# Cross-attention on one Trainium2 core: the audio projection as block products of eleven passes, with the output normalisation spread over the batch

## The chip, the cores and the metric

The kernel runs on one core of one Trainium2 chip. The metric is the device time of a whole execution in microseconds (us); less is better. TensorE (PE) multiplies matrices, VectorE (DVE), ScalarE (ACT) and GpSimd (POOL) do the elementwise work, and SyncE (SP) issues nearly all DMAs from one queue, in order. All numbers are float32.

## What is computed

There are 64 batches. Each has text rows `x` (256 rows of 512) and audio rows `c` (256 rows of 384). The reference, cut to what matters (`H_l` is `x`, `H_a` is `c`):

```python
text_p  = einsum('bld,dh->blh', H_l, W_text)  + b_text     # 512 x 512 weights
audio_p = einsum('bsd,dh->bsh', H_a, W_audio) + b_audio    # 384 x 512 weights
Q = layer_norm(text_p,  g1, beta1)
K = layer_norm(audio_p, g2, beta2)
V = audio_p
alpha = softmax(einsum('blh,bsh->bls', Q, K) / sqrt(512), axis=-1)
H = einsum('bls,bsh->blh', alpha, V)
H = einsum('blh,hk->blk', H, W_out) + b_out
return layer_norm(H + H_l, g_out, beta_out)
```

## The kernel before

The engines run the instructions in the order in which the program lists them; the order of the loop body is written out by hand, and no scheduler reorders it. An engine that waits holds back everything behind it in its own list. Tiles come from pools with a fixed number of buffers, and a new tile waits until the one whose buffer it takes over is done with. [...]

**One batch.** The rows are loaded twice: as rows (`load_rows`, for the residual and as V) and in squares of 32 columns (`load_squares`), which VectorE turns into `xT` and `cT` (`turn_x`, `turn_c`). The text projection is a class `Blocks`: a 2 x 2 block product in seven products instead of eight (Strassen's idea in Winograd's form). GpSimd forms sums of input blocks (`sum_x`, four a batch) and, once at the start, sums of weight blocks (`weight_sums`). TensorE runs the products two to a bank (`products`), and VectorE puts them together (`leave`), one instruction for each product. Each text product takes two matmuls with 256 result columns, so fourteen in all. The audio projection is a plain `Projection`: two row tiles of three matmuls each with 512 result columns (`multiply`), and one eviction for each tile (`evict`). ScalarE squares the rows for the variance, GpSimd makes the inverse root (`scales`), ScalarE scales the rows (`normalise`). The result is stored to DRAM (`store`) and fetched back in squares (`fetch`), VectorE turns it (`turn`), and ScalarE applies the layer norm's weights (`affine`).

The scores are eight matmuls of 256 columns. VectorE takes the row maximum and multiplies it by minus the scale (`maxima`), and ScalarE takes exponentials. These go to DRAM and back (`store_e`, `fetch_e`) and are turned in the next batch (`turn_e`). `context` multiplies them by `c`, six matmuls of 256 columns. The output product uses W_audio times W_out, which is multiplied together once at the start: two tiles of three matmuls of 512 columns. `evict` adds the residual, to which GpSimd has added the output bias (`add_bias`), and takes the statistics; `finish` normalises, two VectorE instructions for each of two row tiles.

**The loop** is a pipeline. In the pass for batch b the scores are those of b, the projections belong to b+2, context and output to b-1 (`last`), and the final normalisation to b-2 (`done`). The input squares of b+3 are turned in the same pass. Batches 0 and 1 are projected ahead of the loop, in the plain form for both sides, and the last two batches end behind it.

Of the kernel before, what the change touches and what calls it, by code (L numbers as in the profile page):

```python
# [9 lines left out]
F32 = mybir.dt.float32  # L10
AF = mybir.ActivationFunctionType
ALU = mybir.AluOpType
# [10 lines left out]
def kernel(  # L23
# [36 lines left out]

    nc = tc.nc
    ctx.enter_context(tc.manual_schedule())
    B, L, D = x.shape
# [10 lines left out]
    work = ctx.enter_context(tc.tile_pool(name="work", bufs=2))  # L76
    small = ctx.enter_context(tc.tile_pool(name="small", bufs=4))
    scratch = ctx.enter_context(tc.tile_pool(name="scratch", bufs=3, space=bass.MemoryType.DRAM))
    p_pj = ctx.enter_context(tc.tile_pool(name="p_pj", bufs=3, space=PSUM))
    p_at = ctx.enter_context(tc.tile_pool(name="p_at", bufs=3, space=PSUM))  # L80
    p_y = ctx.enter_context(tc.tile_pool(name="p_y", bufs=2, space=PSUM))

    def squares(dst, src):
# [68 lines left out]
    def take_columns():  # L152

        ps = p_at.tile([P, P], F32, tag="at", name="ps_v")
        nc.tensor.transpose(ps, vectors, ident)
        nc.scalar.copy(columns, ps[:, : 5 * HC].rearrange("p (n k) -> p n k", n=5))
        return [columns[:, n, :] for n in range(5)]
# [89 lines left out]
        for k in range(n):  # L247
            nc.vector.tensor_scalar(rows[:, k, :], rows[:, k, :], mv[:, k, 0:1], None, ALU.subtract)

    HALF = DC // 2  # L250
    H2 = H // 2

    def weight_sums():

        w = [[wt_sb[:, j * HALF : (j + 1) * HALF, k * H2 : (k + 1) * H2] for k in (0, 1)] for j in (0, 1)]
        t = const.tile([P, 4, HALF, H2], F32, tag="wsum", name="wsum")
        add = nc.gpsimd.tensor_tensor
        add(t[:, 0], w[0][1], w[0][0], ALU.subtract)
        add(t[:, 1], w[1][1], t[:, 0], ALU.subtract)
        add(t[:, 2], w[1][1], w[0][1], ALU.subtract)  # L260
        add(t[:, 3], w[1][0], t[:, 1], ALU.subtract)
        return {1: w[0][0], 2: w[1][0], 3: w[1][1], 4: t[:, 3], 5: t[:, 0], 6: t[:, 1], 7: t[:, 2]}

    def rstd_of(var, n):
        ve = small.tile([P, n], F32, tag="ve", name="ve")
# [5 lines left out]
    class Projection:  # L271


        def __init__(self, name, b, srcT, w_sb, bias, nch, nt):
            self.name, self.b, self.nt, self.nch = name, b, nt, nch
            self.srcT, self.w_sb, self.bias = srcT, w_sb, bias
            self.rows = work.tile([P, nt, H], F32, tag=f"{name}r", name=f"{name}r_{b}")
            self.centred = b > 1
            if not self.centred:
                self.mv = small.tile([P, nt, 2], F32, tag=f"mv{name}", name=f"mv{name}")  # L280
            self.ps = {}
# [96 lines left out]
    class Blocks(Projection):  # L378
# [3 lines left out]

        def __init__(self, b, xT, sums):
            super().__init__("q", b, xT, None, bt_sb, DC, LT)
            part = lambda i, j: xT[:, j * HALF : (j + 1) * HALF, bass.ts(i, P)]
            self.side = {
                1: part(0, 0), 2: part(0, 1), 4: part(1, 1),
                5: sums[:, 0], 6: sums[:, 1], 7: sums[:, 2], 3: sums[:, 3],  # L390
            }

        def products(self, *ns):

            bank = p_pj.tile([P, 2, H2], F32, tag="pj", name="ps_q")
            for j, n in enumerate(ns):
                self.ps[n] = bank[:, j : j + 1, :]
                for k in range(HALF):
                    nc.tensor.matmul(  # L399
                        bank[:, j, :],  # L400
                        lhsT=self.side[n][:, k, :],
                        rhs=blocks_of_wt[n][:, k, :],
                        start=(k == 0),
                        stop=(k == HALF - 1),
                    )

        def leave(self, n):
# [22 lines left out]
    class Attention:  # L430
# [14 lines left out]
                    )  # L445

        def maxima(self):
            mx = small.tile([P, LT], F32, tag="mx", name="mx")
            nc.vector.tensor_reduce(mx, self.sc, AX.X, ALU.max)
            self.nmx = small.tile([P, LT], F32, tag="nmx", name="nmx")  # L450
            nc.vector.tensor_scalar(self.nmx, mx, -scale, None, ALU.mult)

        def exponentials(self):

            self.e = work.tile([P, LT, S], F32, tag="e", name=f"e_{self.b}")
            self.den = small.tile([P, LT], F32, tag="den", name="den")
            for t in range(LT):
                nc.scalar.activation(  # L458
                    self.e[:, t, :],
                    self.sc[:, t, :],  # L460
                    AF.Exp,
                    bias=self.nmx[:, t : t + 1],
                    scale=scale,
                    accum_out=self.den[:, t : t + 1],
                )

# [73 lines left out]
        def scales(self, lo=0, n=LT):  # L540
            self.r = {lo + t: r for t, r in enumerate(rstd_of(self.mv[:, lo : lo + n, 1], n))}

        def finish(self, lo=0, n=LT):
            y = self.y
            for t in range(lo, lo + n):
                nc.vector.scalar_tensor_tensor(  # L546
                    y[:, t, :], y[:, t, :], self.mv[:, t, 0:1], go_sb, ALU.subtract, ALU.mult
                )
                nc.vector.scalar_tensor_tensor(  # L549
                    y[:, t, :], y[:, t, :], self.r[t], beo_sb, ALU.mult, ALU.add  # L550
                )

        def store(self, lo=0, n=LT):
            nc.sync.dma_start(
# [3 lines left out]

    def text(b, xT):
        return Projection("q", b, xT, wt_sb, bt_sb, DC, LT)  # L560

    def sum_x(xT):

        part = lambda i, j: xT[:, j * HALF : (j + 1) * HALF, bass.ts(i, P)]
        s = work.tile([P, 4, HALF, P], F32, tag="xsum", name="xsum")
        add = nc.gpsimd.tensor_tensor
        add(s[:, 0], part(1, 0), part(1, 1), ALU.add)
        add(s[:, 1], s[:, 0], part(0, 0), ALU.subtract)
        add(s[:, 2], part(0, 0), part(1, 0), ALU.subtract)
        add(s[:, 3], part(0, 1), s[:, 1], ALU.subtract)  # L570
        return s

    def audio(b, cT):
        return Projection("k", b, cT, wa_sb, ba_sb, AC, ST)
# [43 lines left out]
    q[0].scales()  # L618
    k[0].fetch()
    g1_sb, be1_sb, g2_sb, be2_sb, bac_sb = take_columns()  # L620
    waT = turn_weights()
    q[0].normalise()
    q[0].store()
# [8 lines left out]
    q[0].fetch()  # L632
    k[1].store()
    blocks[2] = load_squares(2)
    k[0].turn()
    k[0].affine(g2_sb, be2_sb)
    q[1] = text(1, xT.pop(1))
# [15 lines left out]
    fold_evict(1)  # L653
    fold_multiply(2)
    fold_evict(2)
    blocks_of_wt = weight_sums()
    xT[2] = turn_x(2)
    sums = {2: sum_x(xT[2])}
    for v, name in ((bt_sb, "mbt"), (ba_sb, "mba")):
        v = v.rearrange("p (o h) -> p o h", o=1)  # L660
        centre(v, means(v, 1, name), 1)
    blocks[3] = load_squares(3)
    bao_sb = fold_bias(part)
    centre(wa_sb, mean_wa, AC)
    cT[2] = turn_c(2)
    go_sb = row(g_out, "go")
    beo_sb = row(beta_out, "beo")

    done = last = None
    for b in range(B - 2):  # L670
        three = b + 3 < B
        at = Attention(b)
        if b:
            q[b + 1].fetch()
            k[b + 1].normalise()
            k[b + 1].store()
        at.scores()
        if done:
            done.evict(1)
            done.scales()  # L680
        if last:
            last.turn_e()
        at.maxima()
        at.exponentials()
        at.store_e()
        k[b + 1].fetch()
        at.fetch_e()
        if b + 4 < B:
            blocks[b + 4] = load_squares(b + 4)
        rows[b + 1] = load_rows(b + 1)  # L690
        add_bias(b)
        text_2 = q[b + 2] = Blocks(b + 2, xT.pop(b + 2), sums.pop(b + 2))
        text_2.products(1, 2)
        text_2.leave(1)
        text_2.products(6, 5)
        text_2.leave(6)
        text_2.leave(2)
        text_2.leave(5)
        text_2.products(7, 3)
        q[b + 1].turn()  # L700
        q[b + 1].affine(g1_sb, be1_sb)
        at.reciprocals()
        if last:
            last.context()
        if done:
            done.finish()
            done.store()
        text_2.leave(3)
        text_2.leave(7)
        k[b + 2] = audio(b + 2, cT.pop(b + 2))  # L710
        k[b + 2].multiply(0)
        text_2.products(4)
        k[b + 2].evict(0)
        text_2.leave(4)
        text_2.square()
        text_2.scales()
        k[b + 1].turn()
        k[b + 1].affine(g2_sb, be2_sb)
        if three:
            xT[b + 3] = turn_x(b + 3)  # L720
        if last:
            last.start_output()
            last.multiply(0)
        text_2.normalise()
        text_2.store()
        if three:
            sums[b + 3] = sum_x(xT[b + 3])
        k[b + 2].multiply(1)
        if last:
            last.evict(0)  # L730
        if three:
            cT[b + 3] = turn_c(b + 3)
        k[b + 2].evict(1)
        k[b + 2].square()
        k[b + 2].scales()
        if last:
            last.multiply(1)
        done, last = last, at


    at = Attention(B - 2)
    q[B - 1].fetch()
    k[B - 1].normalise()
    k[B - 1].store()
    rows[B - 1] = load_rows(B - 1)
    at.scores()
    done.evict(1)
# [1 line left out]
    last.turn_e()  # L749
    at.maxima()  # L750
    at.exponentials()
    k[B - 1].fetch()
    add_bias(B - 2)
    last.context()
    at.reciprocals()
# [73 lines left out]
```

## Time and profile before

| | |
|---|---|
| time, median of 3 runs | 1482.82 us (1482.72 to 1484.9) |
| the profiled execution | 1483.51 us, span 1481.7 us |
| TensorE busy | 1457.2 us (98%) |
| VectorE busy | 1147.0 us (77%) |
| ScalarE busy | 723.0 us (49%) |
| GpSimd busy | 525.4 us (35%) |
| DMA share of 16 engines, mean moved | 73.8% on the main queue, 217 GB/s |
| granted TensorE clock | 0.997 |

The busy time of an engine is the union of its instructions. TensorE's matmuls overlap in the records and their ends are modelled, so the start of a group is a safer mark than its end. One float32 matmul of the program leaves two records. In lines of the profile, `L399` is a line of the kernel, followed by the engine, the operation, and output and inputs under the program's names.

### The profile page before, as it was taken

The page shows a single profiled execution, that of the slowest core. Times are in us where ns is not written, and L with a number is a line of the kernel's source. Part 1 is how long each engine was busy: PE and PEld are TensorE (multiplying, and loading weights), DVE is VectorE, ACT ScalarE, POOL GpSimd, SP SyncE. Part 2 cuts the span into 40 slices and gives each one's busy share as a digit, 9 for nine tenths or more (in the row PEclk, how much of TensorE's full clock was granted, in tenths as well). Part 3 has the DMA queues.
Part 4 walks back from the last instruction along what each step waited for, and adds up shares of the span by engine and source line. Part 5 has one row for each costly group of instructions (what it writes and reads, how often), then busy time and mean ns, then how long its engine had stood idle before and what let it go on. Part 6 is the DMA issues. An engine that isn't in the chain of part 4 may idle for free.

```text
span 1481.7 us, 18230 instructions
## 1 busy us (share of the span) xinstructions
PE 1457.2 (98%) x5157; PEld 978.4 (66%) x5157; DVE 1147.0 (77%) x1829; ACT 723.0 (49%) x1663; POOL 525.4 (35%) x785
## 2 busy tenths in 40 slices
PE   7999999999999999999999999999999999999997
PEld 3566676676676676676676676676766766766763
DVE  5867877777877877877877877878778778778777
ACT  2444545545545544545545545445445445455452
POOL 1434334334334334334333333343343343343332
PEclk9999999999999999999999999999999999999999
DMA  8777777777778777877777777777777777777752
GB/s 192 179 218 226 217 224 219 223 230 220 220 241 232 221 220 232 227 217 224 223 221 219 216 234 224 218 232 226 218 228 228 213 228 234 212 223 222 227 190 81
DMA packets 450248, 322.27 MB, mean 217 GB/s; under 512 B 154724, under 2 KB 382564, under 8 KB 450148
## 3 DMA queue, kind: packets, MB, share of 16 engines
q1 hardware_dynamic: 449328, 319.79, 73.8%
q10 hardware_dynamic: 820, 1.32, 0.5%
q8 instruction: 41, 0.67, 0.2%
q14 instruction: 59, 0.48, 0.1%
HBM read 204.09 MB, written 116.92 MB: 217 GB/s over the span
## 4 chain that ended last, share of the span: by engine, by line
PE 94%; DMA 2%; DVE 2%; issue 1%; ACT 1%; SPq 0%; POOL 0%; POOLq 0%; DVEq 0%
PE ps_q L399 24%; PE ps_y L521 21%; PE ps_k L286 21%; PE ps_sc L439 14%; PE ps_z L504 11%; PE ps_q L286 1%; PE ps_wao L214 1%; DMA c<-in_ctx_dram 0%; DMA qd<-qr 0%; SPq L87 0%; DMA wt<-in_L_xattn_W_text_dram 0%; DMA bt<-in_L_xattn_b_text_dram 0%; DVE y L549 0%; DVE y L546 0%; DMA ed<-e 0%
## 5 line engine op out<-in xcount | busy, mean ns | idle before, releaser
L286 PE MATMUL ps_k<-wa,cT 128*128 128x512 f32 x768 | 353.0, 596 | 1.0 <-DMA wa<-in_L_xattn_W_audio_dram 1.0
L521 PE MATMUL ps_y<-wao,zT 128*128 128x512 f32 x768 | 350.4, 592 | 1.0 <-ACT zT L511 0.9
L266 POOL TENSOR_SCALAR ve<-var 128x2 f32<-128x2 f32 x124 | 27.1, 218 | 725.4 <-ACT junk L304 725.4
L286 PEld LDWEIGHTS ps_k<-wa,cT 128*128 128x128 f32 x768 | 146.5, 191 | 157.8 <-issue 138.4
L521 PEld LDWEIGHTS ps_y<-wao,zT 128*128 128x128 f32 x768 | 145.6, 190 | 157.8 <-issue 151.4
L414 DVE TENSOR_TENSOR qr<-ps_q,qr 128x512 f32<-128x512 f32 x372 | 184.5, 510 | 76.1 <-PE ps_q L399 71.8
L370 ACT ACTIVATE qT<-qT,columns 128x256 f32<-128x256 f32 x256 | 132.9, 590 | 222.3 <-DVE qT L90 212.6
L439 PE MATMUL ps_sc<-kT,qT 128*128 128x256 f32 x1024 | 233.7, 381 | 3.3 <-ACT kT L370 3.3
L439 PEld LDWEIGHTS ps_sc<-kT,qT 128*128 128x128 f32 x1024 | 195.1, 191 | 58.6 <-issue 27.5
L458 ACT ACTIVATE e<-ps_sc,nmx 128x256 f32<-128x256 f32 x128 | 59.6, 470 | 241.9 <-PE ps_q L399 229.3
L504 PE MATMUL ps_z<-eT,c 128*128 128x256 f32 x768 | 176.3, 379 | 0.7 <-ACT eT L493 0.7
L530 DVE SCALAR_TENSOR_TENSOR y<-ps_y,rden,x 128x512 f32<-128x512 f32 x128 | 93.5, 731 | 103.8 <-PE ps_y L521 102.7
L399 PE MATMUL ps_q<-wsum,xsum 128*128 128x256 f32 x744 | 170.7, 379 | 0.0
L589 POOL TENSOR_TENSOR x<-x,bao 128x512 f32<-128x512 f32 x128 | 160.3, 1274 | 4.6 <-DMA x<-in_x_dram 4.5
L504 PEld LDWEIGHTS ps_z<-eT,c 128*128 128x128 f32 x768 | 145.8, 190 | 21.1 <-ACT eT L493 0.9
L399 PEld LDWEIGHTS ps_q<-wsum,xsum 128*128 128x128 f32 x744 | 141.4, 190 | 19.2
L370 ACT ACTIVATE kT<-kT,columns 128x256 f32<-128x256 f32 x256 | 132.9, 590 | 38.8 <-DVE kT L363 33.7
L268 POOL TENSOR_TENSOR rstd<-ve,nhalf 128x2 f32<-128x2 f32 (+1 forms) x193 | 136.6, 708 | 16.1
L304 ACT ACTIVATE junk<-qr 128x512 f32<-128x512 f32 x124 | 78.1, 630 | 112.5 <-DVE qr L414 112.5
L399 PE MATMUL ps_q<-wt,xT 128*128 128x256 f32 x496 | 117.2, 379 | 0.0
L332 ACT ACTIVATE kr<-kr,rstd 128x512 f32<-128x512 f32 x124 | 82.8, 714 | 70.1 <-POOL rstd L268 70.1
L549 DVE SCALAR_TENSOR_TENSOR y<-y,rstd,beo 128x512 f32<-128x512 f32 x128 | 97.1, 758 | 11.5 <-POOL rstd L268 2.5
(95 smaller groups left out, 1698.1 us busy)
## 6 DMA issues: line engine op xcount, KB each, us to landing
x<-in_x_dram SPq DMA_DIRECT2D x64, 512.0 KB, 5.0
kd<-kr SPq DMA_DIRECT2D x64, 512.0 KB, 3.3
kq<-kd SPq DMA_DIRECT2D x256, 128.0 KB, 2.7
qd<-qr SPq DMA_DIRECT2D x64, 512.0 KB, 4.9
qq<-qd SPq DMA_DIRECT2D x256, 128.0 KB, 2.6
xq<-in_x_dram SPq DMA_DIRECT2D x252, 128.0 KB, 2.8
out_dram<-y SPq DMA_DIRECT2D x63, 512.0 KB, 6.0
c<-in_ctx_dram SPq DMA_DIRECT2D x64, 384.0 KB, 5.3
```

The source lines that it names most:

```text
L268: nc.gpsimd.tensor_tensor(r, ve, nhalf[:, :n], ALU.pow)
L286: nc.tensor.matmul(ps, lhsT=self.srcT[:, k, bass.ts(t, P)], rhs=self.w_sb[:, k, :], start=(k == 0), stop=(k == self.nch - 1),)
L332: nc.scalar.mul(row, row, self.r[t])
L370: nc.scalar.activation(self.T[:, k, :], self.T[:, k, :], AF.Identity, bias=bet[:, k : k + 1], scale=gam[:, k : k + 1],)
L399: nc.tensor.matmul(bank[:, j, :], lhsT=self.side[n][:, k, :], rhs=blocks_of_wt[n][:, k, :], start=(k == 0), stop=(k == HALF - 1),)
L414: add = lambda o, i0, i1: nc.vector.tensor_tensor(o, i0, i1, ALU.add)
L439: nc.tensor.matmul(self.sc[:, t, :], lhsT=self.qT[:, k, bass.ts(t, P)], rhs=self.kT[:, k, :], start=(k == 0), stop=(k == HC - 1),)
L504: nc.tensor.matmul(ps[:, j, :], lhsT=self.c_sb[:, s, bass.ts(lo + j, P)], rhs=self.eT[:, s, :], start=(s == 0), stop=(s == ST - 1),)
L521: nc.tensor.matmul(ps, lhsT=self.zT[:, k, bass.ts(t, P)], rhs=wao_sb[:, k, :], start=(k == 0), stop=(k == AC - 1),)
L530: nc.vector.scalar_tensor_tensor(self.y[:, t, :], self.ps_y.pop(t), self.rden[:, t : t + 1], self.xb[:, t, :], ALU.mult, ALU.add,)
L549: nc.vector.scalar_tensor_tensor(y[:, t, :], y[:, t, :], self.r[t], beo_sb, ALU.mult, ALU.add)
L589: nc.gpsimd.tensor_tensor(xb[:, t, :], xb[:, t, :], bao_sb, ALU.add)
```

## The change

It has four parts.

1. The audio projection from batch 2 on uses `Blocks` as well. The first two of its three chunks of 128 input columns form the 2 x 2 block product, with one matmul for each of the seven products. The third chunk's plain product with `W_audio` has four quarters; each is added by one more matmul to a product that goes to just that quarter of the result (2, 3, 4 and 5). That makes eleven matmuls of 256 columns where there were six of 512. The new `sum_c` makes the sums of input blocks on GpSimd; the sums of weight blocks are made ahead of the loop.
2. `finish` is split into `shift` and `settle` for each row tile, and the four instructions are spread between the maximum and the text evictions.
3. The score's scale goes into the key's layer norm weights ahead of the loop, so that the maximum is negated by the reduction itself and its second small instruction goes.
4. The order changes: all seven text products run ahead of the context, the audio product runs in one piece behind it, and the two output tiles follow each other. The keys of a batch are normalised and stored at the end of the pass instead of at the top of the next, and fetched ahead of the exponentials' store. `add_bias` moves from the top to the middle of the pass. The pools change to four banks for `p_pj` and two for `p_at`.

The core of the diff; the parts of `Blocks` that only take other names are left out.

```diff
-    p_pj = ctx.enter_context(tc.tile_pool(name="p_pj", bufs=3, space=PSUM))
-    p_at = ctx.enter_context(tc.tile_pool(name="p_at", bufs=3, space=PSUM))
+    p_pj = ctx.enter_context(tc.tile_pool(name="p_pj", bufs=4, space=PSUM))
+    p_at = ctx.enter_context(tc.tile_pool(name="p_at", bufs=2, space=PSUM))
...
+    def sum_c(cT):
+        part = lambda i, j: cT[:, j, bass.ts(i, P)]
+        s = work.tile([P, 5, P], F32, tag="csum", name="csum")
+        add = nc.gpsimd.tensor_tensor
+        add(s[:, 0], part(1, 0), part(1, 1), ALU.add)
+        add(s[:, 1], s[:, 0], part(0, 0), ALU.subtract)
+        add(s[:, 2:4], cT[:, 0:3:2, :P], cT[:, 0:3:2, P:], ALU.subtract)
+        add(s[:, 4], part(0, 1), s[:, 1], ALU.subtract)
+        return {
+            1: [part(0, 0)], 2: [part(0, 1), part(0, 2)], 4: [part(1, 1), part(1, 2)],
+            5: [s[:, 0], part(1, 2)], 6: [s[:, 1]], 7: [s[:, 2]], 3: [s[:, 4], s[:, 3]],
+        }
...
         def products(self, *ns):
-            bank = p_pj.tile([P, 2, H2], F32, tag="pj", name="ps_q")
+            bank = p_pj.tile([P, 2, H2], F32, tag="pj", name=f"ps_{self.name}")
             for j, n in enumerate(ns):
                 self.ps[n] = bank[:, j : j + 1, :]
-                for k in range(HALF):
+                pairs = list(zip(self.sides[n], self.weights[n]))
+                for i, (side, w) in enumerate(pairs):
                     nc.tensor.matmul(
...
+                        bank[:, j, :], lhsT=side, rhs=w, start=(i == 0), stop=(i == len(pairs) - 1)
                     )
...
         def maxima(self):
-            mx = small.tile([P, LT], F32, tag="mx", name="mx")
-            nc.vector.tensor_reduce(mx, self.sc, AX.X, ALU.max)
             self.nmx = small.tile([P, LT], F32, tag="nmx", name="nmx")
-            nc.vector.tensor_scalar(self.nmx, mx, -scale, None, ALU.mult)
+            nc.vector.tensor_reduce(self.nmx, self.sc, AX.X, ALU.max, negate=True)
...
+        def shift(self, t):
+            nc.vector.scalar_tensor_tensor(
+                self.y[:, t, :], self.y[:, t, :], self.mv[:, t, 0:1], go_sb, ALU.subtract, ALU.mult
+            )
+
+        def settle(self, t):
+            nc.vector.scalar_tensor_tensor(
+                self.y[:, t, :], self.y[:, t, :], self.r[t], beo_sb, ALU.mult, ALU.add
+            )
...
+    for v in (g2_sb, be2_sb):
+        nc.vector.tensor_scalar(v, v, scale, None, ALU.mult)
...
     blocks[2] = load_squares(2)
+    k[1].fetch()
...
     centre(wa_sb, mean_wa, AC)
+    wa_blocks = weight_sums(wa_sb, 1, "wasum")
+    for n, k2 in ((2, 0), (3, 1), (5, 1), (4, 0)):
+        wa_blocks[n].append(wa_sb[:, 2, k2 * H2 : (k2 + 1) * H2])
     cT[2] = turn_c(2)
+    cs = {2: sum_c(cT[2])}
```

The loop body after the change, for batch b (lines that only stand under `if` for the first and last passes are written without it):

```python
q[b + 1].fetch()
k[b + 1].fetch()
at.scores()
done.evict(1)
done.scales()
done.shift(0)
last.turn_e()
at.maxima()
done.shift(1)
at.exponentials()
at.store_e()
at.fetch_e()
blocks[b + 4] = load_squares(b + 4)
rows[b + 1] = load_rows(b + 1)
q2 = q[b + 2] = Blocks("q", b + 2, xs.pop(b + 2), wt_blocks, bt_sb)
q2.products(1, 2)
q2.leave(1)
done.settle(0)
q2.products(6, 5)
q2.leave(6)
q2.leave(2)
q2.leave(5)
q2.products(7, 3)
q[b + 1].turn()
q[b + 1].affine(g1_sb, be1_sb)
q2.products(4)
q2.leave(3)
q2.leave(7)
q2.leave(4)
at.reciprocals()
last.context()
q2.square()
done.settle(1)
done.store()
q2.scales()
add_bias(b)
k[b + 1].turn()
k[b + 1].affine(g2_sb, be2_sb)
q2.normalise()
q2.store()
k2 = k[b + 2] = Blocks("k", b + 2, cs.pop(b + 2), wa_blocks, ba_sb)
k2.products(1, 2)
k2.leave(1)
k2.products(6, 5)
k2.leave(6)
k2.leave(2)
k2.leave(5)
k2.products(7, 3)
k2.leave(3)
k2.leave(7)
k2.products(4)
k2.leave(4)
k2.square()
k2.scales()
last.start_output()
last.multiply(0)
xT[b + 3] = turn_x(b + 3)
xs[b + 3] = sum_x(xT.pop(b + 3))
cT[b + 3] = turn_c(b + 3)
cs[b + 3] = sum_c(cT.pop(b + 3))
k2.normalise()
k2.store()
last.evict(0)
last.multiply(1)
```

## The prediction

> **What bounds the kernel now.** I read the busy shares first, then TensorE in order of time, then the same batch on VectorE, then the waits of the first and last batches.
>
> ```profile
> PE 1457.2 (98%) x5157; PEld 978.4 (66%) x5157; DVE 1147.0 (77%) x1829; ACT 723.0 (49%) x1663; POOL 525.4 (35%) x785
> L286 PE MATMUL ps_k<-wa,cT 128*128 128x512 f32 x768 | 353.0, 596 | 1.0 <-DMA wa<-in_L_xattn_W_audio_dram 1.0
> ```
>
> TensorE is busy for 98%, with hardly any wait in front of it. That alone could be modelled ends, so here is its timeline for one batch (start, duration, instruction, records):
>
> ```profile
> 721.44 3.62 PE L439 MATMUL ps_sc<-kT,qT 128*128 128x256 f32 x16
> 724.89 1.89 PE L399 MATMUL ps_q<-wt,xT 128*128 128x256 f32 x8
> 726.62 2.75 PE L399 MATMUL ps_q<-wsum,xsum 128*128 128x256 f32 x12
> 729.21 1.03 PE L399 MATMUL ps_q<-wt,xsum 128*128 128x256 f32 x4
> 730.07 2.75 PE L504 MATMUL ps_z<-eT,c 128*128 128x256 f32 x12
> 732.66 2.74 PE L286 MATMUL ps_k<-wa,cT 128*128 128x512 f32 x6
> 735.24 1.03 PE L399 MATMUL ps_q<-wsum,xT 128*128 128x256 f32 x4
> 736.10 2.74 PE L521 MATMUL ps_y<-wao,zT 128*128 128x512 f32 x6
> 738.68 2.74 PE L286 MATMUL ps_k<-wa,cT 128*128 128x512 f32 x6
> 741.25 2.74 PE L521 MATMUL ps_y<-wao,zT 128*128 128x512 f32 x6
> 743.83 2.54 PE L439 MATMUL ps_sc<-kT,qT 128*128 128x256 f32 x11
> ```
>
> Read the starts, not the durations. A batch takes 743.83 - 721.44 = 22.39 us with no idle time anywhere. The same period runs from the start at 94.61 to the one at 1437.81: 1343.20 / 60 = 22.387. One program matmul leaves two records. From start to start, 12 narrow records (256 columns) take 2.59 us, 0.216 each, and 6 wide ones (512 columns) take 2.575, 0.429 each. Call a 256-wide matmul (two narrow records) a pass: a batch has 8 for scores, 14 text, 6 context, 12 audio, 12 output, 52 in all, at 0.43 us. For 60 of 64 batches only the number of passes counts, as long as nothing else becomes late.
>
> **The change part by part.**
>
> *Passes.* From batch 2 on (62 batches) the audio projection goes from 6 wide matmuls to 11 narrow ones. Before: 12 wide records x 0.429 = 5.15 us. After: 22 narrow records x 0.216 = 4.75. Saved: 0.40 us; by the mean pass (22.387/52) it would be 0.43. I take 0.41, a period of 21.98. 62 x 0.41 = 25.4 us (24.8 to 26.7).
>
> [...] The row decides: 0.216 against 0.429, at a granted clock of 1.00. The text products already run as narrow matmuls with fresh weights each, and their weight loads (0.190 us a record) lie under the 0.216.
>
> *VectorE.* Removed per batch: two audio evictions (2 x 0.685) and the small negation of the maximum, L451 (1.07): 2.44 us. Added: seven evictions of quarter and half results. The text ones took (184.5 + 42.1)/62 = 3.65 us a batch (both L414 groups). In the 57 batches from 117.00 to 1392.90 VectorE was busy 1005.06/57 = 17.63 us a batch; it becomes 18.8 of 21.98, 86%. The output normalisation keeps its four instructions, only spread out.
>
> *GpSimd.* Added per batch: four sums for audio, three of 128 columns and one of 256. Sums of 512 took 1.27 us and of 256 0.73; that puts 128 at about 0.46, so 2.1 us. From 460.83/57 = 8.1 to 10.2 us of 21.98.
>
> *Does the new order keep TensorE fed?* I lay one batch out, t = 0 at its first score matmul. TensorE: scores to 3.45, text products to 9.49 (pairs at 5.18, 6.90, 8.63), context to 12.08, audio pairs to 13.38, 14.67, 15.96 and the last to 16.83, output to 19.40 and 21.98. VectorE in its new order, with the durations above and its waits on those ends: second eviction with statistics 0.2-1.9; shift of row 0 to 2.6; exponentials' transpose 3.3; maximum (waits for the scores) 3.65-4.35; shift 1 to 5.1; text 1 5.35-6.05; settle 0 to 6.8; text 6, 2, 5 7.1-8.5; query transpose 9.7; text 3, 7, 4 11.2; settle 1 12.0; key transpose 13.2; audio 1 13.55-14.25, 6 from 14.85, 2 and 5 to 16.25, 3, 7, 4 to 17.7; input transposes to 19.8; first output eviction to 21.45. It closes with about 2.7 us idle.
>
> Margins, each from this layout. PSUM: the first audio bank needs text 2 out (7.9 against 12.08); the second context tile, in a pool cut from three to two, needs the exponentials done (5.8 against 11.2). ScalarE: affine of q 9.7-11.8, context copies to 12.9 (wanted 16.83), text squares 14.5, affine of k 16.6 (wanted 21.98), text normalise 17.9, audio squares 19.5, then GpSimd's root to 20.5, audio normalise 21.9. GpSimd: text sums 20.5-23.4 (the first pair wanted at 27.2), audio sums to 25.5 (wanted at 35.4), root for the output 26.5 (wanted by settle 0 at 28.0). SP, in order: the audio store, issued at 22.3, is now ahead of the next query fetch, which also needs the query store landed (17.9 + 4.9 = 22.8); four query issues to 24.7, landing 2.6 later, 27.3, wanted at 30.5. The key fetch behind it waits for that store to land (3.3): 25.6-27.5, landed 30.2, wanted at 34.0. The exponentials' store is ready at 27.8, so SP is free for it; its fetch now follows the store directly and holds SP for the 2.2 us landing, ahead of input loads that are used a batch later. The thinnest margin is 1.5 us, in front of VectorE; those in front of TensorE are about 4 us or more. I cost the whole reordering at 0.
>
> [...] The normalisation steps have two SBUF inputs. First the rows, from the last batches (GpSimd's bias sum and VectorE):
>
> ```profile
> 1446.40 2.94 POOL L589 TENSOR_TENSOR x<-x,bao 128x512 f32<-128x512 f32 x2 [3.13 <-DMA x<-in_x_dram]
> ...
> 1446.59 1.63 DVE L549 SCALAR_TENSOR_TENSOR y<-y,rstd,beo 128x512 f32<-128x512 f32 x1
> 1448.15 1.75 DVE L546 SCALAR_TENSOR_TENSOR y<-y,mvy,go 128x512 f32<-128x512 f32 x1
> 1449.93 0.75 DVE L549 SCALAR_TENSOR_TENSOR y<-y,rstd,beo 128x512 f32<-128x512 f32 x1
> ```
>
> Beside GpSimd sums these two take 1.63 and 1.75 us; the next, alone, 0.75. In the steady batches of before all four stand where GpSimd is idle (705 to 715). In my layout shift 0 (1.9-2.6) meets the audio sums that run until 25.5 - 21.98 = 3.5; the other three fall into GpSimd's pause from 4.5 to 14.5. By the rows one collision costs 0 to 1.0 us, and 0.3 of idle time follows it before the maximum and 0.25 before text 1: nothing reaches TensorE. [...]
>
> *First batches.*
>
> ```profile
> PE ps_sc L439 <- ACT kT L370: 2.4, 1, 2.4
> 70.00 5.53 PE L439 MATMUL ps_sc<-kT,qT 128*128 128x256 f32 x16 [2.45 <-ACT kT L370]
> 62.68 2.01 SPq L87 DMA_DIRECT2D kq<-kd  x4
> DVE kT L363 <- DMA kq<-kd: 2.6, 1, 2.6
> ```
>
> The second scores stand still 2.45 us and then need 5.53 for 3.45: 4.5 us, because the fetch of the key rows was issued at 62.68, behind the exponentials' store. It now goes out before the loop, at about 46.3, so that data is there. But it is queued ahead of the query store (47.64) and fetch (56.04), which move by up to 2 us, and the query transpose (61.25) with them; the seven audio evictions then push the next sums. GpSimd's weight and input sums for audio, 5 us, start when the weights are centred (55.9) and end at 61, wanted at 63.5. I expect 2.5 us gained (0 to 4.4).
>
> *Last batches.* With two banks the second context tile waits for the exponentials, +0.5 us, which themselves come 1.1 earlier without L451; -0.3 in all (-1 to +1).
>
> **Sum.** 25.4 + 2.5 + 0.3 = 28.2. The profiled execution took 1483.51 us (span 1481.7 and 1.8 around it): 1455.3. The median of the runs shown, 1482.82, lies 0.7 below: 1454.6.
>
> **The rivals.**
>
> B, *part of it comes back as late data*: one of the margins is thinner than I drew (a landing of 6 us for the query store, as at 72.68 in the start-up, in place of 4.9; DMA queues at 76% in this stretch). TensorE then stops 0.1 to 0.35 us a batch: 1461 to 1476. For: the SP queue is issuing some 12 of 22 us and now has waits at its head. Against: margins of 3.2 and 3.8 us for those fetches, and 4 more behind VectorE.
>
> [...]
>
> D, *no gain*: narrow audio records cost 5.15/22 = 0.234 us, because the short accumulations (three of one matmul) change destination at every matmul. Then only the start-up gain is left, 1480. Against: text products change destination every second matmul at 0.216.
>
> **How the numbers follow.** Forecast 0.80, B 0.10, C 0.07, D 0.03. The forecast's bounds are 62 x (0.40 to 0.43), 0 to 4.4 and -1 to +1: 1450 to 1459. The range reaches into B: 1450 to 1467, leaving out half of B, C and D. About 0.2% (3 us) can be told from no change. Faster by more: forecast and B, 0.90; within: D, 0.03; slower: C, 0.07.
>
> **What would show it.** Right: starts of the scores 21.98 us apart with no idle time of TensorE; 22 records of the audio product in 4.75 us; VectorE near 86% a batch, GpSimd 10.2 us; L451's work gone; the second scores less than 2.5 us late. Wrong: waits of text or audio matmuls on VectorE or GpSimd in every batch (B), all normalisation steps above 1.5 us (C), audio records 0.23 us apart (D).

## The result, and the profile after

| | before | after |
|---|---|---|
| time, median | 1482.77 us (1481.93 to 1484.9, 4 runs) | 1473.2 us (1471.16 to 1476.08, 4 runs) |
| ratio | | 0.9935, 95% interval 0.9915 to 0.9955 |
| span of the profiled execution | 1481.7 us | 1471.0 us |
| granted TensorE clock | 0.997 | 0.995 |

The change gains 0.65%, about a third of the forecast. The profiled execution was to have a span of 1481.7 - 28.2 = 1453.5 us and has 1471.0, so 17.5 us are missing. The busy shares of after show nothing of it:

```profile
PE 1437.6 (98%) x5777; PEld 1097.4 (75%) x5777; DVE 1213.2 (82%) x2077; ACT 697.1 (47%) x1663; POOL 692.6 (47%) x1037
```

TensorE is at 98% as before. The starts of the scores show where the time went. The span falls into three parts:

| part, by the starts of scores | before | forecast | after | after against forecast |
|---|---|---|---|---|
| to the third scores | 94.61 us | 91.3 | 100.64 | +9.3 |
| third scores to second last, 60 periods | 1343.20 | 1319.0 | 1326.76 | +7.8 |
| second last scores to the end | 43.89 | 43.6 | 43.6 | 0 |

Forecast for the first part: 2.5 us, and two passes of the loop at 0.41. For the second: 60 x 0.403 less. Rounding and the last digit of the forecast make the rest of the 17.5.

So there are two losses, one in the loop and one in the start-up. A batch that nothing disturbs is as forecast. This is TensorE's timeline of after, one batch (start, duration, instruction, records):

```profile
675.94 3.62 PE L463 MATMUL ps_sc<-kT,qT 128*128 128x256 f32 x16
...
688.03 1.46 PE L427 MATMUL ps_k<-wa,cT 128*128 128x256 f32 x6
...
692.77 5.31 PE L542 MATMUL ps_y<-wao,zT 128*128 128x512 f32 x12
697.92 1.24 PE L463 MATMUL ps_sc<-kT,qT 128*128 128x256 f32 x5
```

697.92 - 675.94 = 21.98 us, and the 22 audio records take 692.77 - 688.03 = 4.74. But of the 60 periods twelve are longer, 22.11 to 23.46, all of them among the first forty; the others are 21.98 or 21.99. The waits of after name the releaser:

```profile
DVE qT L91 <- DMA qq<-qd: 151.0, 61, 6.9
PE ps_k L427 <- DVE qr L438: 11.0, 11, 3.1
```

(Engine, output and line, what it waited for: us in total, times, longest.) Two of TensorE's eleven waits, 6.0 of the 11.0 us, lie in the start-up, the other nine in the loop. In nearly every batch VectorE stands in front of the query transpose until the query fetch has landed, 2.5 us on average. That transpose is listed ahead of the text evictions 3, 7 and 4; so when it is very late, the bank that the third audio pair takes over is not yet empty, and TensorE stops. One such place, the transpose on VectorE and then the wait on TensorE:

```profile
666.13 1.25 DVE L91 STREAM_TRANSPOSE qT<-qq 128x1024 f32<-128x1024 f32 x1 [3.22 <-DMA qq<-qd]
```

```profile
668.56 0.67 PE L427 MATMUL ps_k<-wasum,csum 128*128 128x256 f32 x2 [0.35 <-DVE qr L438]
```

The question is why the fetch is late. Here is one round of SP's queue in after:

```profile
661.86 1.80 SPq L88 DMA_DIRECT2D qq<-qd  x4
663.76 1.87 SPq L88 DMA_DIRECT2D kq<-kd  x4
665.73 0.40 SPq L494 DMA_DIRECT2D ed<-e  x1
668.81 1.78 SPq L88 DMA_DIRECT2D eq<-ed  x4
670.69 1.87 SPq L88 DMA_DIRECT2D xq<-in_x_dram  x4
672.66 1.88 SPq L88 DMA_DIRECT2D cq<-in_ctx_dram  x4
674.65 0.39 SPq L106 DMA_DIRECT2D x<-in_x_dram  x1
675.14 0.41 SPq L107 DMA_DIRECT2D c<-in_ctx_dram  x1
675.64 0.42 SPq L580 DMA_DIRECT2D out_dram<-y  x1
676.15 0.42 SPq L373 DMA_DIRECT2D qd<-qr  x1
678.36 0.36 SPq L373 DMA_DIRECT2D kd<-kr  x1
```

The next query fetch goes out at 683.40. Read the starts and look for the gaps. There are two long ones: 665.73 to 668.81, in which SP waits for the exponentials' store to land before it can fetch them, and 676.15 to 683.40, in which it waits for the query store to land. The 14.3 us ahead of the query store hold no long gap for an engine. SP's waits over the whole span say the same:

```profile
SPq L88 <- DMA qd<-qr: 312.3, 63, 6.7
SPq L88 <- DMA ed<-e: 165.4, 62, 3.1
...
SPq L373 <- ACT qr L363: 5.1, 2, 4.0
```

SP has waited for the query rows of ScalarE twice in 64 batches; they are always there first. (It waits for the key rows, 73.9 us in all, but that is the pause from 676.57 to 678.36, inside the landing.) Its other waits for engines are below 1 us each, apart from a few at the two ends of the run. The long wait for the query store alone says little, for SP has it in before too; but there it also stands for ScalarE, for the query rows and for the exponentials, in most batches:

```profile
SPq L87 <- DMA qd<-qr: 291.8, 63, 7.7
SPq L342 <- ACT qr L332: 116.4, 53, 4.5
SPq L473 <- ACT e L458: 96.4, 45, 4.0
```

In after these pauses are gone. So hardly anything that the engines do speeds SP up: its list and the landings in it form a round of their own, 22.16 us on average over the 58 fetches from 105.65 to 1390.8, where TensorE could do 21.98.

### The profile page after: what moved, and what is told of

Same layout as the page of the kernel before. It is cut to its first block, busy times and chain, and to the rows that moved or that the text cites. A ratio compares the mean times of both kernels' runs of the same rounds, so it can differ in the third digit from the quotient of the medians.

```text
span 1471.0 us, 20463 instructions
## 1 busy us (share of the span) xinstructions
PE 1437.6 (98%) x5777; PEld 1097.4 (75%) x5777; DVE 1213.2 (82%) x2077; ACT 697.1 (47%) x1663; POOL 692.6 (47%) x1037
## 2 busy tenths in 40 slices
DMA packets 450260, 322.41 MB, mean 219 GB/s; under 512 B 154724, under 2 KB 382564, under 8 KB 450148
## 5 line engine op out<-in xcount | busy, mean ns | idle before, releaser
L542 PE MATMUL ps_y<-wao,zT 128*128 128x512 f32 x768 | 340.3, 592 | 0.0
L438 DVE TENSOR_TENSOR kr<-ps_k,kr 128x512 f32<-128x512 f32 x372 | 185.3, 512 | 24.7 <-DVE kr L438 0.9
L91 DVE STREAM_TRANSPOSE qT<-qq 128x1024 f32<-128x1024 f32 x64 | 79.7, 1245 | 151.0 <-DMA qq<-qd 151.0
L427 PE MATMUL ps_q<-wtsum,xsum 128*128 128x256 f32 x744 | 170.7, 379 | 0.0
L427 PE MATMUL ps_k<-wa,cT 128*128 128x256 f32 x620 | 164.6, 380 | 0.0
L427 PEld LDWEIGHTS ps_q<-wtsum,xsum 128*128 128x128 f32 x744 | 141.4, 190 | 19.2
L427 PEld LDWEIGHTS ps_k<-wa,cT 128*128 128x128 f32 x620 | 118.2, 191 | 16.2
L427 PE MATMUL ps_k<-wasum,csum 128*128 128x256 f32 x372 | 102.6, 385 | 11.0 <-DVE qr L438 11.0
```

Of the source, the lines that this page charges most:

```text
L91: nc.vector.transpose(dst.rearrange("p k (b j) -> p b k j", j=SQ), src.rearrange("p b (k i) -> p b k i", k=chunks),)
L427: nc.tensor.matmul(bank[:, j, :], lhsT=side, rhs=w, start=(i == 0), stop=(i == len(pairs) - 1))
L438: add = lambda o, i0, i1: nc.vector.tensor_tensor(o, i0, i1, ALU.add)
L542: nc.tensor.matmul(ps, lhsT=self.zT[:, k, bass.ts(t, P)], rhs=wao_sb[:, k, :], start=(k == 0), stop=(k == AC - 1),)
```

## The experiments

Two theories stood at first. *Queue:* the order of the DMAs on SP (the exponentials' fetch straight behind its store, and at the start a load that SP waits for) costs the missing time, and TensorE's new order is sound. *Engines* (VectorE theory in the expectations): the new passes or the new order on VectorE and GpSimd cost it, because VectorE is too full (82%) or a bank is emptied late, and mending the queue gives little; by it e1 changes nothing. Times are medians; ratios are against the kernel before in the same series, where it took 1484.18 (e1 to e4), 1484.54 (e5 to e8) and 1486.13 us (e9 to e11).

**e1_rows_early: the start-up.** SP's queue in the start-up of after, and SP's wait for `go`:

```profile
46.43 11.38 SPq L88 DMA_DIRECT2D kq<-kd  x4
57.91 0.40 SPq L373 DMA_DIRECT2D qd<-qr  x1
61.54 1.78 SPq L88 DMA_DIRECT2D qq<-qd  x4
```

```profile
SPq L88 <- DMA go<-in_L_xattn_g_out_dram: 9.7, 1, 9.7
```

Four issues that elsewhere take 1.87 us take 11.38: SP stands 9.7 us in the middle of the key fetch, and the wait is put down to the load of `go`, which has nothing to do with keys. ScalarE issues that load only at 52.67, behind its other work. What ties the fetch to that load is not shown. Behind the key fetch stands the query store, 47.64 before and 57.91 now. The experiment moves the two row loads up:

```diff
     bo_sb = row(b_out, "bo")
+    go_sb = row(g_out, "go")
+    beo_sb = row(beta_out, "beo")
...
-    go_sb = row(g_out, "go")
-    beo_sb = row(beta_out, "beo")
```

> The changed kernel, with the two broadcast loads go and beo issued on ScalarE's queue right behind bo instead of behind the last fold copy. Queue theory (SP's in-order queue holds the batches back, in two places): at the start SP stood 9.7 us in front of the second key fetch, put down to go, and the query store of batch 1 went out at 57.9 instead of 47.7. With go early that wait goes: third scores at about 92 to 94 instead of 100.6, so 1473.2 - 8 = 1465 (1463 to 1468); the 7.8 us of waits spread over batches 8 to 43 stay. [...]

Measured: 1480.11 us (1472.92 to 1481.66, 9 runs), 0.996 [0.9944, 0.9976]. The start-up is as forecast, the total is not. SP in the start-up of e1:

```profile
48.34 1.86 SPq L88 DMA_DIRECT2D kq<-kd  x4
50.31 0.39 SPq L373 DMA_DIRECT2D qd<-qr  x1
```

The wait is gone, the query fetch goes out 7.2 us earlier (54.38), and the third scores start at 91.2 instead of 100.64. What has gone are two stops of TensorE in after, one of 2.88 us at 68.45 and this one (behind them the granted clock was 0.50, for some 6.0 and 3.4 us, as the last section shows):

```profile
91.60 1.19 PE L427 MATMUL ps_k<-wasum,csum 128*128 128x256 f32 x2 [3.11 <-DVE qr L438]
```

But the loop of e1 then loses more than after's: 60 periods average 22.33 instead of 22.11, and TensorE waits for text evictions 20 times in it instead of 9. SP's round is 22.38 us. The row loads explain the start-up alone; a start that is 9 us better is lost again where SP sets the pace.

**e2_fetch_late: the loop.** The exponentials' fetch goes behind the input loads of the pass, so that SP issues those while the store lands.

```diff
         at.store_e()
-        at.fetch_e()
...
         rows[b + 1] = load_rows(b + 1)
+        at.fetch_e()
```

> The changed kernel, with the fetch of the exponentials moved behind load_squares and load_rows in SP's queue, so that SP does not stand 3.1 us for the exponentials' store to land. Queue theory: SP's own round (22.1 us for a TensorE period of 21.98) becomes some 19 to 20 us; all scores from batch 3 on start 21.98 us apart, the query fetch is ahead of VectorE, VectorE's wait for it (2.5 us a batch) goes: 1473.2 - 7.8 = 1465.4, a little less if the stall of batch 1 shrinks too (1462 to 1466). VectorE theory: VectorE has the same work, so the same waits, 1472 to 1475.

Measured: 1457.84 us (1456.83 to 1458.53), 0.982 [0.9806, 0.9835]: more than was expected of it. All periods from the third scores on are 21.98. The third scores themselves start at 94.38, 6.3 us earlier than in after, although SP still waits for `go` (11.61 us for the four issues): part of the start-up's loss was the same queue, in the passes that follow (TensorE's second stop is 0.41 us instead of 3.11). The longest of SP's waits in e2:

```profile
SPq L373 <- ACT qr L363: 206.3, 61, 4.7
```

Now SP waits for ScalarE in each batch, 3.4 us for the query rows, so TensorE's batch sets the pace and SP has slack. The query transpose waits 6.0 us in all, twice, instead of 151.0. Both kernels move 322.41 MB and give VectorE and GpSimd the same work, so that neither the amount of data nor a full engine was what cost these 15 us. And the store itself lands sooner, with the same 512 KB. These are the rows of the DMA issues (issue, count, size, median us to landing) of after and then of e2:

```profile
qd<-qr SPq DMA_DIRECT2D x64, 512.0 KB, 7.2
```

```profile
qd<-qr SPq DMA_DIRECT2D x64, 512.0 KB, 3.0
```

In after the store is issued 0.5 us behind the output store and the two row loads (512 + 512 + 384 KB, issued within 1.5 us). In e2 SP stands for ScalarE at that place, and those 1.4 MB have had more than 3 us to move. I read this as a state with two sides: an SP that is late issues the store straight behind the big transfers, the store lands late, and SP stays late. No run here shows a kernel going from one side to the other.

**e3_both: e1's and e2's edits together.**

> Both edits together. Queue theory: the two losses are in different places and add up: 1473.2 - 8 - 8 = 1457 (1453 to 1460), no TensorE wait from batch 3 on. VectorE theory: 1472 to 1475.

Measured: 1455.08 us (1454.98 to 1455.99), 0.9804 [0.9789, 0.9818], span 1453.2. Third scores at 91.15, all periods 21.98. This is the forecast of 1454.6, with two mends of the queue. Neither edit touches what TensorE, VectorE or GpSimd compute. No kernel here is faster.

**e9_fetch_behind_squares: a smaller move.** The exponentials' fetch goes behind the squares' loads only, so that the 1.4 MB ahead of the query store stay as in after.

```diff
         at.store_e()
-        at.fetch_e()
         if b + 4 < B:
             blocks[b + 4] = load_squares(b + 4)
+        at.fetch_e()
```

> The changed kernel with the exponentials' fetch moved only behind load_squares, not behind the row loads; no byte is moved behind or ahead of the projection stores. The eight issues of load_squares (3.8 us) cover the landing of the exponentials' store, so SP's round loses the wait of some 2.7 us and falls to about 19.4. Queue theory: no waits of TensorE from batch 3 on, as with the fetch behind all loads: 1459 (1456 to 1463). If it was the order of the bytes that helped there (stores landing in 3 instead of 7 us because something else stands in front of them), the time stays above 1465.

Measured: 1458.21 us (1457.87 to 1458.71), 0.9808 [0.978, 0.9836]: as e2. Its SP waits 198.3 us for the query rows, and the store lands in 3.4. The 1.4 MB straight ahead of the store and their order are those of after; what differs is the place of the 256 KB fetch further ahead, and the pause of some 3.3 us in front of the store that comes with it.

**e8_loads_behind: the big transfers out of the store's way.** A second reading of the 7.2 us was that the 1.4 MB ahead are the whole fault. Here they are issued behind the two projection stores, and the exponentials' fetch stays where after has it.

```diff
-        rows[b + 1] = load_rows(b + 1)
...
-            done.store()
...
         k2.store()
+        rows[b + 1] = load_rows(b + 1)
+        if done:
+            done.store()
```

> The changed kernel with the row loads and the output store (1.4 MB) moved behind the two projection stores in SP's queue; the fetch of the exponentials stays where the change put it, with its wait of some 3 us. If it is SP's whole round that counts, the query store lands some 4 us sooner after its issue (3 instead of 7.2 us) and the loads' issue fills that wait: round under 20 us, no waits of TensorE from batch 3 on, 1465 (1458 to 1467). If the wait for the exponentials' store is what does it by itself, 1471 to 1475.

Measured: 1556.22 us (1554.05 to 1559.16), 1.049 [1.0473, 1.0507]: a clear miss, on the other side. The query store lands in 3.2 us as expected. But now the fetches stand behind the big transfers. DMA issues of e8:

```profile
qq<-qd SPq DMA_DIRECT2D x256, 128.0 KB, 6.7
...
ed<-e SPq DMA_DIRECT2D x62, 256.0 KB, 4.3
```

The query pieces take 6.7 us to land (2.6 in after), the exponentials' store 4.3 (3.2), and SP waits 232.7 us for that store, 68.3 for output stores and 31.0 for row loads. (The last two are not data that the fetches need; what ties the fetches to these transfers is not shown.) TensorE's period is 23.4 us on average, and so is SP's round, where TensorE needs 21.98. Here the engines are part of the round: SP also waits 169.4 us for the key rows of ScalarE,

```profile
SPq L373 <- ACT kr L363: 169.4, 62, 3.2
```

which are late in turn, because late query data (VectorE's query transpose waits 241.2 us for it) holds up the text evictions and TensorE's audio products behind them (72.5 us, 58 times). No landing can be judged alone: moved out of one wait, the same bytes lie in front of the next.

**e4_passes_alone and e7_passes_four_banks: the eleven passes in the old order.** The kernel before gets the audio block products and `sum_c`, and keeps its own order, its negation of the maximum and its three banks for projections.

```diff
-        k[b + 2] = audio(b + 2, cT.pop(b + 2))
-        k[b + 2].multiply(0)
+        k2 = k[b + 2] = Blocks("k", b + 2, cs.pop(b + 2), wa_blocks, ba_sb)
+        k2.products(1, 2)
+        k2.products(6, 5)
         text_2.products(4)
-        k[b + 2].evict(0)
+        k2.leave(1)
+        k2.leave(6)
+        k2.leave(2)
+        k2.leave(5)
         text_2.leave(4)
...
-        k[b + 2].multiply(1)
+        k2.products(7, 3)
+        k2.products(4)
...
-        k[b + 2].evict(1)
+        k2.leave(3)
+        k2.leave(7)
+        k2.leave(4)
```

> The kernel before, with only the audio projection as eleven passes (its sums, products and seven evictions) in the old order of the loop, old queues, old pools, finish in one piece and the maximum in two instructions. Queue theory: SP's order is that of before, whose round had room, so each batch takes 21.98 us and the start is that of before: 1482.8 - 62 x 0.405 = 1457.7 (1456 to 1461). VectorE theory: VectorE has 1.07 us a batch more to do than in the changed kernel, so the waits are at least as long: 1473 or more.

Measured: 1491.16 us (1487.19 to 1502.0, 10 runs), 1.0055 [1.0031, 1.0078]: slower than before, a miss. Two things add up. The undisturbed period is 22.19, because the last text product waits for a bank (TensorE for text evictions, 18.4 us, 25 times); and the mean period is 22.47, with SP waiting for stores (302.6 us for the query store, 291.8 in before; 160.1 for the key store, 69.4 in before). e7 takes the banks as a cause out: four for projections and two for scores and context, as after has them.

```diff
-    p_pj = ctx.enter_context(tc.tile_pool(name="p_pj", bufs=3, space=PSUM))
-    p_at = ctx.enter_context(tc.tile_pool(name="p_at", bufs=3, space=PSUM))
+    p_pj = ctx.enter_context(tc.tile_pool(name="p_pj", bufs=4, space=PSUM))
+    p_at = ctx.enter_context(tc.tile_pool(name="p_at", bufs=2, space=PSUM))
```

> The kernel before with the eleven passes in the old order, now with four banks for projections and two for scores and context. In the three-bank form the last text product waited in every batch for a bank (period 22.19 at best) and the mean period was 22.47. Bank theory: without that wait each batch takes 21.98, 1461. Queue theory: the 0.2 us a batch go, but the rest stays, since SP waits for the landings of the query, key and exponentials' stores as it did: period 22.2 to 22.3, 1476 (1470 to 1482).

Measured: 1493.76 us (1486.73 to 1494.82), 1.0061 [1.0041, 1.008]. The undisturbed period is 21.98 now, and the time is no better: the mean is 22.53. TensorE's waits in the loop are now put down to ScalarE's copies of the context (21.5 us, 35 times), which stand behind the late queries in ScalarE's list. The first of SP's waits in e7:

```profile
SPq L87 <- DMA qd<-qr: 329.0, 63, 6.6
```

The banks are real, but they are not what is left. That it is SP, whose round is no shorter for having faster engines beside it (22.57 us here), is for e10 to show.

**e10_passes_fetches_late: the old order with SP's list mended.** e7 with the row loads of e1, the key fetch behind the squares' loads and the exponentials' fetch behind the row loads.

```diff
-        k[b + 1].fetch()
-        at.fetch_e()
         if b + 4 < B:
             blocks[b + 4] = load_squares(b + 4)
+        k[b + 1].fetch()
         rows[b + 1] = load_rows(b + 1)
+        at.fetch_e()
```

> The eleven passes in the old order of compute with four banks (1493.8 us), now with SP's list mended: go and beo early, the key fetch behind load_squares and the exponentials' fetch behind the row loads, so that SP stands for neither landing. Queue theory: what kept this order at 22.6 us a batch was SP, so it comes to 21.98 to 22.1: 1461 (1457 to 1470). Compute-order theory: the old order of products and evictions cannot carry eleven passes, 1480 or more.

Measured: 1464.24 us (1461.68 to 1464.44), 0.9845 [0.9821, 0.987]: within what was expected. All periods are 21.98. So the old order of the engines carries the eleven passes too: from e7 to e10 29.5 us come from the place of DMAs in two queues. Of the 9 us that are left to e3, 7.4 lie in the start-up: the second and third scores follow after 19.77 and 24.96 us (14.25 and 22.83 in e3), with TensorE waiting 5.4 us for the keys.

**e6_six_wide: the passes for themselves.** e3 with the plain audio projection, six matmuls of 512 columns and no audio sums.

```diff
-        k2 = k[b + 2] = Blocks("k", b + 2, cs.pop(b + 2), wa_blocks, ba_sb)
+        k2 = k[b + 2] = audio(b + 2, cT.pop(b + 2))
+        k2.multiply(0)
+        k2.evict(0)
+        k2.multiply(1)
+        k2.evict(1)
...
-            cs[b + 3] = sum_c(cT.pop(b + 3))
```

> The third kernel with the audio projection as six wide matmuls again (two evictions, no audio sums), all else as there: measures the passes by themselves. By the records 62 x 0.405 = 25.1 us more, period 22.39: 1480.2 (1478.5 to 1482). If narrow records were dearer than half a wide one and other parts of the new order had paid for the 1455, the difference is smaller than 20 us.

Measured: 1479.14 us (1478.18 to 1480.74), 0.9966 [0.9956, 0.9976], all periods 22.39. Against e3 the eleven passes are worth 1479.14 - 1455.08 = 24.1 us; the periods say about the same, 62 x (22.39 - 21.98) = 25.4. The wide passes in the new order are still 5.4 us faster than the kernel before in the same series, with the same period; 4.1 us of that is an earlier third score (90.5 against 94.6).

**e5_finish_whole and e11_maximum_in_two: what the small parts are worth.** e5 is e3 with the normalisation in one piece at the place of the second `settle`; e11 is e3 with the maximum and its multiplication by minus the scale in two instructions again.

```diff
-            done.shift(0)
...
-            done.shift(1)
...
-            done.settle(0)
...
-            done.settle(1)
+            done.finish()
```

> The third kernel (go early and the fetch of the exponentials late, 1455.1 us) with the output normalisation put back into one piece at the place of the second settle. Queue theory: VectorE has room (the evictions wait for TensorE there, not the other way), so the spreading was worth nothing: 1455 (1454 to 1457). Theory that the spreading is what keeps VectorE in time: waits of TensorE come back, 1459 or more.

```diff
+            mx = small.tile([P, LT], F32, tag="mx", name="mx")
-            nc.vector.tensor_reduce(self.nmx, self.sc, AX.X, ALU.max, negate=True)
+            nc.vector.tensor_reduce(mx, self.sc, AX.X, ALU.max)
+            nc.vector.tensor_scalar(self.nmx, mx, -scale, None, ALU.mult)
```

> The third kernel (1455.1 us) with the maximum and its scaling in two instructions again and the scale in the exponentials. VectorE gets up to 1.07 us a batch more, 19.9 of 21.98. By VectorE's waits for TensorE there (some 2.1 us a batch) it has room: 1455.5 (1454.5 to 1457.5). If VectorE were already at its end: 1460 or more.

Measured: e5 1455.5 us, 0.981 [0.9793, 0.9826]; e11 1456.65 us (1455.56 to 1458.84), 0.98 [0.9775, 0.9825]. Both are as expected, no more than 1.6 us from e3 and with the same period: TensorE doesn't notice either. The spreading and the shorter maximum are no part of the gain once SP's list is mended.

## Why the prediction was right in its passes and wrong in its queue

- **Passes: right.** 22 records in 4.74 us, a period of 21.98, 24.1 us by e6 against 25.4 forecast. The row's price for a narrow record, half a wide one (0.216 us against 0.429), held: 4.74 / 22 = 0.215.
- **VectorE and GpSimd: right.** From 117 to 1400 VectorE was busy 1083.21 us of 1283, 84% (86% forecast), and GpSimd 622.39 us in some 58 periods, 10.7 a batch (10.2).
- **Normalisation beside GpSimd's sums: right that it costs little, wrong on who meets whom.** I let one shift of a batch meet the audio sums; both do. Tile 0's takes 902 ns in the median (727 in before) and tile 1's 835 (744), and none exceeds 1034: 0.27 us a batch in all, where I had 0 to 1.0 for one of them. The other loser is GpSimd's sum L287, 785 ns in the median where I had 460. The sign of C (slower, at 0.07), all normalisation steps above 1.5 us, did not come: their medians in after are 840 ns (`shift`) and 750 (`settle`).
- **Last batches: right in the sum**, 0.3 us; its two terms were not measured apart.
- **The reordering at 0: wrong**, by 7.8 us in the loop; this is the step "SP, in order". There I drew the query store going out as soon as its rows are ready, at t = 17.9, landing 4.9 us later, and the query fetch going out at 22.8 for a transpose at 30.5. With SP mended (e3) this came true: store at 17.1, fetch at 21.8, transpose at 30.5 (medians over passes 5 to 59). In after the store goes out at 22.4, the fetch at 29.6, and the transpose starts at 33.9. Of the 7.7 us between the two fetches, 3.3 are rows that are late behind the late queries of the pass, 2.0 is SP still busy with its list, and 2.4 is a longer stretch from the store to the fetch. I followed SP for one batch from t = 22.3 with landings taken from the rows of before:

```profile
kd<-kr SPq DMA_DIRECT2D x64, 512.0 KB, 3.3
...
qd<-qr SPq DMA_DIRECT2D x64, 512.0 KB, 4.9
...
ed<-e SPq DMA_DIRECT2D x62, 256.0 KB, 2.2
```

  In after they are 7.0, 7.2 and 3.2. The rows of before held for a queue that stood for ScalarE's query rows and exponentials (116.4 and 96.4 us in all), and so issued the query store later behind the big transfers: in one batch 3.8 us behind the output store (715.14 to 718.92), where after issues it 0.5 us behind (675.64 to 676.15). I moved the waits and kept the landings. Nor did I close the round; but that by itself would not have shown the loss. In the batch shown it is 14.3 us from the query fetch to the query store and 7.25 for its landing, 21.5 (22.16 on average) for a batch of 21.98; with the landings of before the same sum is about 18. So the terms that failed are the landings, and the hold of the exponentials' fetch (2.2 us, at no cost in the forecast) that takes the pause away in which they would be short. e2 and e9 take this hold out, the query store lands in 3.0 and 3.4 us, and every wait of TensorE in the loop goes.
- **First batches: wrong**, by 9.3 us; the step is "which move by up to 2 us". The query store moved by 10.3 us, 47.64 to 57.91. The wait for `go` was in the trace of before (8.0 us), where it stood in front of the query fetch alone; moving the key fetch into it put the query store behind it too. TensorE then stopped twice, for 6.0 us, and ran behind these stops at half clock for some 9.4 us (granted 0.50 from 68 to 74 and from 92 to 94, and in part in the next 2 us), by an estimate 4.7 more; it also began 0.6 us later than in before. The forecast had left 2.0 of the 4.5 us that before loses in its one stop: 6.0 + 4.7 + 0.6 - 2.0 = 9.3. With the row loads early (e1) the third scores start at 91.2, against 91.3 by the forecast; this agreement is in part luck, since no stop is left in front of the second scores and the first start 1.0 us later than in before.
- **Rival B** was the right mechanism at 0.10: late data through SP, a query store that lands late, and TensorE standing 7.8 / 60 = 0.13 us a batch in the range that it named. It had no word of the start-up, and I gave it too little because I counted the margins with landings that no longer held, as if the loop would start afresh in each batch.

Open stays why SP's round is not the same everywhere: 22.24 us over the first 41 rounds of after, 21.96 over the next 17 (where TensorE stops no more), and 22.38 in e1, whose runs spread over 9 us. All of them consist of issues and landings; which transfers meet which was not taken apart. Nor is it known why e1, with the better start, has the slower loop.

## What to carry to other kernels

Sum an in-order DMA queue as a round: all of its issues, and every landing that stands in front of an issue, once around; if that is near the batch (here 22.16 us for a batch of 21.98), look at the queue as at a bound like an engine, however wide its margins look in a single pass. The sum is only as good as its landings: take landing times with what was issued just ahead of them, and where a change takes away a pause in front of a store, reckon with a later landing (here 7.2 us where before had 4.9). A DMA that must itself stand for something, moved forward in the list, made everything that it passed stand with it here: the key fetch stood 9.7 us, and the query store behind it moved from 47.64 to 57.91.

## What the runs showed of the hardware

- The same 512 KB store landed in 7.2 us straight behind 1.4 MB (after), in 3.0 and 3.4 us with a pause of some 3 us between them (e2, e9), in 3.2 us without the 1.4 MB ahead of it (e8), and in 4.9 us in before, where the pause was 2.2 us on average in 53 batches. 128 KB fetches landed in 2.6 us (after), and in 6.7 us behind 1.4 MB (e8).
- A DMA on SP's queue waited 9.7 us (after) by the profile for one that ScalarE issues and whose data it does not need; with that load issued early (e1) the wait is gone. What ties the two together stays open.
- After a stop of 2.88 us TensorE's matmuls ran at half pace for some 6 us:

```profile
68.45 1.19 PE L427 MATMUL ps_k<-wasum,csum 128*128 128x256 f32 x2 [2.88 <-DVE qr L438]
69.44 1.91 PE L427 MATMUL ps_k<-wa,csum 128*128 128x256 f32 x4
```

  Four records took 1.70 us from start to start instead of 0.86. The windows of TensorE for this stretch (busy time, granted clock, DMA share and GB/s) show the granted clock:

```profile
68.00:70.00 2.00, 1.55 (x4) 0.50 0.96 221
...
74.00:76.00 2.00, 2.00 (x9) 0.88 0.83 229
```

  The granted clock is at half behind the stop and back some 6 us after TensorE resumed, so that this stop cost about twice its length: 2.88 us, and by an estimate half of those 6.0. Behind the stop of 3.11 us at 91.60 it is at half for some 3.4 us (0.50 from 92 to 94), as behind the stop of 2.45 us in before (0.50 from 72 to 74). The length of a stop does not decide this alone. In e9 the stop at the same place has full pace behind it, four records in 0.86 us:

```profile
68.28 0.67 PE L427 MATMUL ps_k<-wasum,csum 128*128 128x256 f32 x2 [2.72 <-DVE qr L438]
68.79 1.03 PE L427 MATMUL ps_k<-wa,csum 128*128 128x256 f32 x4
69.65 0.59 PE L427 MATMUL ps_k<-wasum,cT 128*128 128x256 f32 x2
```

  So has a stop of 3.21 us in e8 (at 89.26; four records in 0.86 us), while behind one of 1.95 us there (at 1260.68) two records take 0.85 us, half pace, from 1262.45 to 1263.30 and again to 1264.15. The stops of 0.35 us (at 668.56) and 1.23 us (at 823.92) in the loop of after cost no clock: the records behind them are 0.216 us apart, at 1.00 granted. What decides it stays open.
- The multiplication of the maximum, two elements per partition, took 1103 ns in before and 169 in e11, both in the median. In before 63 of the 64 overlap GpSimd's bias sum of 512 columns (one: 725.82 to 726.92, beside 724.40 to 726.89), and the one that does not (at 1458.89) takes 0.17 us; in e11, where the bias sum stands in the middle of the pass, the longest takes 1095.
